# A gated message-passing kernel on one core: edge chunks of growing size, three packed lists, and six quads fetched from x

## The chip, the core and the metric

The kernel runs on one core of one Trainium2 chip. The metric is device time in microseconds, as a median of runs. Lower is better.

## The reference

There are 12,500 nodes with 128 features and 400,000 edges. The edges are sorted by destination, and the destinations are denser at small numbers. Each edge has a length. An edge counts only if its length is at most 10; the lengths are drawn up to 56, so most edges drop out.

```python
rbf = exp(-(d[:, None] - centers)**2 / (2 * width**2))           # 50 centers, width 0.1
cut = 0.5 * (cos(pi * d / 10) + 1) * (d <= 10)
W   = (silu(rbf @ fw1 + fb1) @ fw2 + fb2) * cut[:, None]          # a filter for each edge
messages = (x[src] @ pw + pb) * W
agg = segment_sum(messages, dst)
h   = x + (silu(agg @ mw1 + mb1) @ mw2 + mb2)
out = layernorm(x + h)
```

Everything is float32.

## The kernel before

The engines are VectorE (DVE), ScalarE (ACT), TensorE (PE), GpSimd (POOL) and SyncE (SP, which here only issues DMAs). The order of each engine's instructions is the order in which the kernel is written down (`manual_schedule`); no scheduler moves anything. Each engine then runs its own queue in order, and waits where it needs another one's result.

**The projection.** `x @ pw + pb` is computed once for all nodes, in 25 tiles of 512 rows, and written to a table `proj` in DRAM. For each tile SP loads x (`load_x`), PE transposes it (`turn`, L469), ACT copies the transpose out of PSUM (L471), PE multiplies it (`project`, L239 for the bias and L242), ACT copies the result (L480), and SP stores it. The bias is a sum of three bfloat16 parts, which DVE makes in `in_parts` (L229 to L233).

**Packing.** The edges that count must be brought together. The list of 400,000 edges is cut into 5 chunks. A chunk is 128 rows of 625 consecutive edges. `pack(c)` is a generator that writes down DVE instructions and yields their estimated microseconds, so that the kernel can put them between others. For one chunk DVE marks the edges that drop out (`drop`, L302), counts them along each row (`gone`, L305), and has PE add up the counts of the rows in front (`at`, L314 and L316), to know where each row's edges begin. Then it moves the edges that stay to the left, by a power of two in each of ten steps: `go` (L345) is a mask, `nodes` (L351 to L358) are node numbers and `r_d` (L360) are lengths. The front of each row becomes `line` (L365 to L380, `CAP` = 160 edges wide). POOL scatters all lines with one indirect DMA into `packed` in DRAM (L382). Neighbouring rows overlap there, so even rows go to one list and odd rows to a second; both start as zeros, and are joined by a bitwise OR. The joined list comes back as `pair` (L393). From it DVE and PE make, for each packed edge, its source (`srci`), its destination inside a window of 128 nodes (`dl`), its cutoff (`cut`) and the first node of its window (`base_i`); the lengths go to `near_d`. This is the pair stage, L401 to L456.

**The main loop.** The packed edges are worked off in 141 quads of 512. `QB` says which quads come from which chunk. For one quad:

- `fetch`: POOL issues four indirect DMAs of 128 rows from `proj` into `got` (L490). There are 8 such buffers. A fetch is written down `AHEAD` = 3 quads ahead of its use.
- `radial_of` loads the lengths (SP), `basis` makes the radial functions (ACT), `first` multiplies them by fw1 (PE, L529), `tanh` (ACT) and `silu` (DVE, L542) follow, for two quads at a time; `second` multiplies by fw2 (PE, L554).
- `message`: DVE multiplies the filter by the fetched rows (L560).
- `place`: DVE builds a one-hot matrix weighted with the cutoff (four `hot`, L568).
- `sum_up`: PE multiplies messages by it (L577), and `add` adds two windows to `aggT` (DVE, L595). `aggT` holds the whole sum in SBUF and is cleared by POOL in 25 memsets (L153).

Between these steps the loop writes down packing of later chunks, by a budget of 1.3 estimated microseconds after an even quad and 2.5 after an odd one. A yield of -3 or -1 means that the chunk rests for that many quads, while a DMA is under way. From quad 70 on, tiles of nodes that are complete get the last layers (`nodes`), and `finish` does the rest after the loop.

**Before the loop.** POOL writes the zeros of `packed` (four DMAs, L146) and clears 3,500 columns of `aggT` (7 memsets). DVE makes the parts of pb and then packs chunk 0; the 18 other memsets stand on POOL behind chunk 0's scatter. PE and ACT do the projection meanwhile. The first fetch needs both the sources of chunk 0 and the whole table `proj`.

The functions that the diff touches, with the line numbers of the profile:

Of the kernel before, what the change touches and what calls it, by code (L numbers as in the profile page):

```python
# [30 lines left out]
CAP = 160  # L31


QB = (0, 26, 54, 81, 109, 141)
NC_ = len(QB) - 1
NQ = QB[-1]
AHEAD = 3
GOT = 8
# [7 lines left out]
def kernel(  # L46
# [40 lines left out]
    R = E // (NC_ * P)  # L87
# [3 lines left out]
    assert H == P and E == NC_ * P * R and E % P == 0 and W <= N <= 1 << SB  # L91
    assert CAP <= R < 1 << (32 - RB - SB) and 2 * MW % P == 0
# [32 lines left out]
    def load_rows(c):  # L125

        raw[c] = []
        for name, ap, dt in (("r_d", edge_weight, I32), ("r_dst", dst, I32), ("r_src", src, I32)):
            t = work.tile([P, R], dt, name=name, bufs=2)
            v = ap[c * P * R:(c + 1) * P * R].rearrange("(r l) -> r l", r=P)  # L130
            nc.sync.dma_start(t, v if ap is not edge_weight else v.bitcast(I32))
            raw[c].append(t)
# [9 lines left out]
    zero_i = keep.tile([P, 2 * MW // (4 * P)], I32, name="zero_i")  # L142
    nc.gpsimd.memset(zero_i, 0)
    packed = dram.tile([2, MW], I32, name="packed")
    for k in range(4):
        nc.gpsimd.dma_start(packed.rearrange("s (k w) -> (s k) w", k=P // 2)  # L146
                            .rearrange("p (q w) -> p q w", q=4)[:, k], zero_i)
    aggT = keep.tile([P, N], F32, name="aggT")

    def clear(a, b):  # L150

        for n0 in range(a, b, 500):
            nc.gpsimd.memset(aggT[:, n0:min(n0 + 500, b)], 0.0)  # L153

    clear(0, 3500)
# [50 lines left out]
    side_i = keep.tile([P, 1], I32, name="side_i")  # L206
    nc.vector.tensor_scalar(side_i, part_i, 1, None, op0=OP.bitwise_and)
    side = keep.tile([P, 1], F32, name="side")
    nc.vector.tensor_scalar(side, side_i, float(MW), None, op0=OP.mult)
# [77 lines left out]
    bits = (R - 1).bit_length()  # L287
    LB = RB + SB

    def rowed(dt, name, n=R, bufs=1):  # L290
        return work.tile([P, n], dt, name=name, bufs=bufs)

    def pack(c):

        if c + 1 < NC_:
            load_rows(c + 1)
        r_d, r_dst, r_src = raw[c]
# [5 lines left out]
        yield 0.6  # L303
        gone = rowed(F32, "gone")
        nc.vector.tensor_tensor_scan(gone, drop, drop, 0.0, op0=OP.add, op1=OP.max)  # L305
        yield 1.4
# [4 lines left out]
        yield 0.9  # L311
# [10 lines left out]
        yield 0.6  # L322
        relc = rowed(F32, "drop")
        nc.vector.tensor_scalar(relc, rel, -127.5, None, op0=OP.add)
        yield 0.4
        nc.vector.tensor_reduce(span[:, c:c + 1], relc, AX.X, OP.max, apply_absolute_value=True)
        yield 0.7
# [4 lines left out]
        yield 0.3  # L332
# [3 lines left out]
        yield 0.7  # L336
        nc.vector.scalar_tensor_tensor(nodes, step, LB, nodes, op0=OP.logical_shift_left,
                                       op1=OP.bitwise_or)
        yield 0.7
        for b in range(bits):  # L340
            k = 1 << b

            n = min(R - k, CAP + sum(1 << j for j in range(b + 1, bits)))
            go = rowed(I32, "go")
            nc.vector.tensor_scalar(go[:, :n + k], nodes[:, :n + k], 31 - LB - b, 31,  # L345
                                    op0=OP.logical_shift_left, op1=OP.arith_shift_right)
            yield 0.4
            m = go[:, k:n + k]
            if b < bits - 1:
                after = rowed(I32, "nodes", bufs=2)  # L350
                nc.vector.scalar_tensor_tensor(after[:, :n + k], go[:, :n + k], -1,  # L351
                                               nodes[:, :n + k], op0=OP.bitwise_xor,
                                               op1=OP.bitwise_and)
                yield 0.7
                nc.vector.copy_predicated(after[:, :n], m, nodes[:, k:n + k])  # L355
                nodes = after
            else:
                nc.vector.copy_predicated(nodes[:, :n], m, nodes[:, k:n + k])  # L358
            yield 0.7
            nc.vector.copy_predicated(r_d[:, :n], m, r_d[:, k:n + k])  # L360
            yield 0.7
# [15 lines left out]
        line = work.tile([P, CAP, 2], I32, name="line", bufs=2)  # L377
# [8 lines left out]
        if c == 0:  # L386
            clear(3500, N)
        yield -3
# [3 lines left out]
        pair = work.tile([64, 2, 512], I32, name="pair", bufs=1)  # L392
# [4 lines left out]
        def paired(dt, name):  # L397
            return work.tile([64, 256], dt, name=name, bufs=1)[:np_]

        length = paired(I32, "length")  # L400
        nc.vector.tensor_tensor(length, pair[:np_, 0, 1::2], pair[:np_, 1, 1::2], OP.bitwise_or)  # L401
# [3 lines left out]
        nc.vector.tensor_tensor(two, pair[:np_, 0, ::2], pair[:np_, 1, ::2], OP.bitwise_or)  # L405
# [17 lines left out]
        def to_places(k, f, to):  # L423
            for j in range(2):
                nc.tensor.transpose(tp[:, k, j, :np_], f[:, j * P:(j + 1) * P], ident[:np_, :np_])
            nc.vector.tensor_copy(to[:, p0:p0 + np_, :].rearrange("p r j -> p j r"),
                                  tp[:, k, :, :np_])

        to_places(0, f_src, srci)
        part = paired(I32, "part")  # L430
# [32 lines left out]
    def turn(t0):  # L463
        r = rows(t0)
        n = sum(r)
        xp = bank("pu")
        x4 = x_sb.pop(t0)
        for k, m in enumerate(r):
            nc.tensor.transpose(xp[:, k * P:k * P + m], x4[:m, k, :], ident[:m, :m])  # L469
        xT = work.tile([P, 4 * P], F32, name="xT", bufs=3)  # L470
        nc.scalar.copy(xT[:, :n], xp[:, :n])  # L471
        xT_of[t0] = xT
# [9 lines left out]


    d_of, rbf_of, ph_of, t_of, s_of, pu_of, got_of, pa_of, hot_of = ({} for _ in range(9))

    def fetch(q, idx=None):
        got = work.tile([P, QT, H], F32, name="got", bufs=GOT)
        for j in range(QT):
            i = srci[:, 2 * q + j // 2, j % 2:j % 2 + 1] if idx is None else idx[:, j:j + 1]
            nc.gpsimd.indirect_dma_start(  # L490
                out=got[:, j, :], out_offset=None, in_=proj,
                in_offset=bass.IndirectOffsetOnAxis(ap=i, axis=0))
        got_of[q] = got
# [12 lines left out]
    def radial_of(o, eng=None):  # L506
        if 2 * o < NQ:
            assert all(chunk_of(q) in stored for q in quads(o))
            radial(o, [near_d[2 * q:2 * q + 2].rearrange("(o p) e -> o (p e)", o=1)
                       for q in quads(o)], eng)  # L510

    def chunk_of(q):
        return max(c for c in range(NC_) if QB[c] <= q)
# [269 lines left out]

    in_parts("pb", pb_f)
    tiles = list(range(0, NT, 4))
    turn(tiles[0])
    turn(tiles[1])
    at_t = 0.0
    weights = None
    for k, t0 in enumerate(tiles):  # L790
        if k + 6 < len(tiles):
            load_x(tiles[k + 6])
        if k == 4:
            weights = load_weights()
        project(t0)
        if k + 2 < len(tiles):
            turn(tiles[k + 2])
        t = 1.9 * (k + 1)
        while at_t < t:
            c = 0 if not rest[0] else 1  # L800
            v = next(chunks[c])
            if v < 0:
                rest[c] = -v
            else:
                at_t += 1.15 * v
    fb2_f, mb1_f, mb2_f, fw2_sb, mw1_sb, mw2_sb = weights
    rest[0] = 0
    assert not rest[1]
    advance(0, 0.1)
    fw2_h = keep.tile([H, H], F32, name="fw2_h")  # L810
    nc.vector.tensor_scalar(fw2_h, fw2_sb, 0.5, None, op0=OP.mult)
    advance(0, 1.15)
    for o in range(2):
        radial_of(o, nc.gpsimd)
    for q in range(AHEAD):
        fetch(q)
    for o in range(2, 4):
        radial_of(o)
    while 0 in todo:
        advance(0, 1.0)  # L820
    basis(0)
    first(0)
    in_parts("fb2", fb2_f)
# [10 lines left out]
    for q in range(NQ):  # L834
        nodes(q)
        if q + AHEAD < NQ:
            assert min(todo, default=NC_) > chunk_of(q + AHEAD)
            fetch(q + AHEAD)
        if q % 2 == 0:
            radial_of(q // 2 + 4)  # L840
            if 2 * (q // 2 + 1) < NQ:
                tanh(q // 2 + 1)
        else:
            if q + 3 < NQ:
                first((q + 3) // 2)
            if q + 5 < NQ:
                basis((q + 5) // 2)
        if q + 1 < NQ:
            second(q + 1)
        msg = message(q)  # L850
        sum_up(q, msg)
        if q:
            base_of(q - 1, (0,))
        if q + 1 < NQ:
            place(q + 1)
        if q:
            base_of(q - 1, (1,))
            add(q - 1)
        if q % 2 == 0 and 2 * (q // 2 + 1) < NQ:
            silu(q // 2 + 1)  # L860
        left = 1.3 if q % 2 == 0 else 2.5
        for c in list(todo[:2]):
            if rest[c]:
                rest[c] -= 1
            elif left > 0:
                left = advance(c, left)
        if not todo and "mw2" not in late:
            late["mw2"] = mw2_h = keep.tile([H, H], F32, name="mw2_h")
            nc.vector.tensor_scalar(mw2_h, mw2_sb, 0.5, None, op0=OP.mult)
            in_parts("mb1", mb1_f)  # L870
            in_parts("mb2", mb2_f)
            count()
        elif not todo and total is None:
            total = nc.values_load(bad_i[0:1, 0:1], min_val=0, max_val=2 * E)
# [86 lines left out]
```

## Time and profile before

| | us |
|---|---|
| median of 3 runs (lowest, highest) | 834.27 (833.3, 835.0) |
| the profiled execution, its own time | 830.76 |
| its span, first to last instruction | 829.0 |
| DVE busy | 679.6 (82%) |
| PE busy | 588.0 (71%) |
| POOL busy | 578.6 (70%) |
| ACT busy | 257.6 (31%) |

The span is what the profile divides up; 1.8 us of the execution lie around it. Busy time leaves out the issue of DMAs by SP and the pause that POOL makes between two gathers, so a POOL that is never free shows some 75% in the loop.

### The profile page before, as it was taken

What the parts mean: (1) busy time and instruction counts of PE and PEld (TensorE: products, weight loads), DVE (VectorE), ACT (ScalarE), POOL (GpSimd) and SP (SyncE); (2) the same over time, 40 slices, a digit from 0 to 9 for tenths busy, and PEclk for the clock granted to TensorE, in tenths of its full rate; (3) what the DMA queues carried; (4) which work ended last, traced back from release to release, by engine and by line L of the source; (5) the groups of instructions that cost most, each with busy time, mean ns of one, the idle gap of its engine ahead of it and who ended that gap; (6) DMA issues with size and microseconds to landing.
All of it is one profiled execution on the core that took longest, in us unless ns stands there. A gap on an engine that the chain in (4) does not pass through costs nothing.

```text
span 829.0 us, 11346 instructions
## 1 busy us (share of the span) xinstructions
PE 588.0 (71%) x3356; PEld 449.8 (54%) x3356; DVE 679.6 (82%) x1822; ACT 257.6 (31%) x397; POOL 578.6 (70%) x613
## 2 busy tenths in 40 slices
PE   4792766666667766776767687787877876867862
PEld 4680545455555555555555465555655664646651
DVE  7967899989999998999968888777867667667774
ACT  2454322132222322232222233523434424521521
POOL 3045777777777777777777777777777777777750
PEclk9995788878887788768896799998999988999887
DMA  8994324232153323233333442722623623632421
GB/s 245 265 309 122 96 64 128 72 103 76 49 151 77 90 73 80 58 97 88 88 83 92 102 118 77 195 66 78 181 77 89 169 80 87 171 99 52 122 61 41
DMA packets 85700, 90.62 MB, mean 109 GB/s; under 512 B 13623, under 2 KB 64851, under 8 KB 85632
## 3 DMA queue, kind: packets, MB, share of 16 engines
q1 hardware_dynamic: 66464, 49.95, 21.1%
q0 software_dynamic: 18912, 39.77, 19.4%
q8 instruction: 28, 0.46, 0.2%
q14 instruction: 40, 0.33, 0.1%
q10 hardware_dynamic: 256, 0.11, 0.1%
HBM read 74.71 MB, written 15.07 MB: 108 GB/s over the span
## 4 chain that ended last, share of the span: by engine, by line
DVE 33%; POOL 17%; PE 16%; DMA 15%; issue 14%; DVEq 3%; ACT 1%; SPq 1%; POOLq 0%; ACTq 0%
POOL got L490 16%; DMA got<-proj,srci 11%; DVE hot L568 8%; DVE s L542 4%; PE pa L577 4%; DVE msg L560 3%; DVE aggT L595 3%; PE ph L529 3%; PE pu L554 3%; DMA x<-in_x_dram 3%; DVEq L585 2%; DVE r_d L360 2%; PE pa L242 1%; PE ms L242 1%; DVE st L629 1%
## 5 line engine op out<-in xcount | busy, mean ns | idle before, releaser
L490 POOL DMA_INDIRECT got<-proj,srci x564 | 553.8, 982 | 171.9 <-issue 146.6
L577 PE MATMUL pa<-hot,msg 128*128 128x128 f32 x1128 | 184.6, 315 | 107.1 <-DVE msg L560 106.8
L577 PEld LDWEIGHTS pa<-hot,msg 128*128 128x128 f32 x1128 | 164.3, 224 | 121.4 <-DVE msg L560 121.3
L554 PEld LDWEIGHTS pu<-fw_h,s 128*128 128x128 f32 x1128 | 176.2, 223 | 12.0 <-issue 5.1
L554 PE MATMUL pu<-fw_h,s 128*128 128x128 f32 x1128 | 174.8, 306 | 0.0
L568 DVE TENSOR_SCALAR hot<-iota_n,dl,cut 128x128 f32<-128x128 f32 x564 | 158.0, 356 | 0.8 <-PE pa L577 0.6
L535 ACT ACTIVATE t<-ph 128x1024 f32<-128x1024 f32 (+1 forms) x71 | 71.8, 1012 | 268.5 <-PE ph L529 255.0
L529 PE MATMUL ph<-rbf,w_sb 51*128 51x512 f32 x282 | 101.3, 791 | 63.9 <-DVE s L542 53.3
L560 DVE TENSOR_TENSOR msg<-pu,got 128x512 f32<-128x512 f32 x141 | 96.3, 683 | 60.4 <-DMA got<-proj,srci 49.1
L542 DVE SCALAR_TENSOR_TENSOR s<-t,ph 128x1024 f32<-128x1024 f32 (+1 forms) x71 | 85.7, 1207 | 6.8 <-ACT t L535 6.7
L595 DVE TENSOR_TENSOR aggT<-aggT,pa 128x128 f32 x282 | 79.9, 283 | 7.5 <-PE ms L607 2.3
L529 PEld LDWEIGHTS ph<-rbf,w_sb 51*128 51x128 f32 x282 | 27.8, 224 | 85.3 <-issue 52.6
L551 PE MATMUL pu<-fb_b,ones_b 96*128 96x512 bf16 x141 | 61.7, 438 | 0.0
L609 ACT ACTIVATE zt<-ms 128x512 f32<-128x512 f32 (+1 forms) x25 | 14.6, 587 | 150.3 <-PE ms L607 150.3
L519 ACT ACTIVATE rbf<-d,rbf_bias,rbf_scale 128x512 f32<-128x512 f32 (+1 forms) x71 | 57.1, 804 | 0.2
L668 ACT ACTIVATE x<-x,by,rs 128x128 f32<-128x128 f32 x91 | 37.3, 482 | 59.4 <-DVE by L638 59.4
L551 PEld LDWEIGHTS <-ones_b 96*128 96x128 bf16 x141 | 14.9, 105 | 73.7 <-issue 73.2
L520 ACT ACTIVATE rbf<-rbf 128x512 f32<-128x512 f32 (+1 forms) x71 | 44.7, 630 | 2.2
L351 DVE SCALAR_TENSOR_TENSOR nodes<-go,nodes 128x625 int32<-128x625 int32 x45 | 36.5, 810 | 1.3
L360 DVE COPY_PREDICATED r_d<-go,r_d 128x624 int32<-128x624 int32 (+9 forms) x50 | 36.9, 739 | 0.0
L355 DVE COPY_PREDICATED nodes<-go,nodes 128x624 int32<-128x624 int32 (+8 forms) x45 | 35.9, 798 | 1.2
L626 DVE SCALAR_TENSOR_TENSOR x<-x,ms 128x512 f32<-128x512 f32 x23 | 15.8, 686 | 24.9 <-PE ms L242 24.9
(159 smaller groups left out, 501.1 us busy)
## 6 DMA issues: line engine op xcount, KB each, us to landing
d<-near_d SPq DMA_DIRECT2D x137, 128.0 KB
x<-in_x_dram SPq DMA_DIRECT2D x48, 256.0 KB
got<-proj,srci POOLq DMA_INDIRECT x564
proj<-hp SPq DMA_DIRECT2D x24, 256.0 KB
out_dram<-x SPq DMA_DIRECT2D x24, 256.0 KB
r_d<-in_edge_weight_dram SPq DMA_DIRECT2D x5, 312.5 KB
r_dst<-in_dst_dram SPq DMA_DIRECT2D x5, 312.5 KB
r_src<-in_src_dram SPq DMA_DIRECT2D x5, 312.5 KB
```

Source lines behind the costliest of these rows:

```text
L360: nc.vector.copy_predicated(r_d[:, :n], m, r_d[:, k:n + k])
L490: nc.gpsimd.indirect_dma_start(out=got[:, j, :], out_offset=None, in_=proj, in_offset=bass.IndirectOffsetOnAxis(ap=i, axis=0))
L519: nc.scalar.activation(rbf[:u], d[:u], AF.Square, bias=rbf_bias[:u], scale=rbf_scale[:u])
L529: nc.tensor.matmul(ph[:, h, :], w1_sb[p0:p0 + KR], rbf[p0:p0 + KR], start=True, stop=True)
L535: nc.scalar.activation(t[:, :n], ph[:, :n], AF.Tanh, scale=0.5)
L542: nc.vector.scalar_tensor_tensor(s[:, :n], t_of.pop(o)[:, :n], 1.0, ph[:, :n], op0=OP.add, op1=OP.mult)
L551: nc.tensor.matmul(pu, ones_b[:, :P], bias_b["fb2"].rearrange("k j f -> k (j f)"), start=True, stop=False)
L554: nc.tensor.matmul(pu[:, j * H:(j + 1) * H], s[:, j * P:(j + 1) * P], fw2_h, start=False, stop=(j == QT - 1))
L560: nc.vector.tensor_mul(msg, pu_of.pop(q).rearrange("p (j f) -> p j f", j=QT), got_of.pop(q))
L568: nc.vector.tensor_scalar(hot[:, j, :], iota_n[:, :W], dl[:, at[0], at[1]], cut[:, at[0], at[1]], op0=OP.is_equal, op1=OP.mult)
L577: nc.tensor.matmul(pa[:, k * W:(k + 1) * W], msg[:, j, :], hot[:, j, :], start=(j % 2 == 0), stop=(j % 2 == 1))
L595: nc.vector.tensor_add(to, to, pa[:, k * W:(k + 1) * W])
```

## The change

- The 5 equal chunks become 6, of 250, 450, 550, 625, 625 and 625 edges a row (`ROWS`), with lines of 80, 128 and then 160 edges (`CAPS`). `QB` gives them 10, 20, 24, 27, 28 and 32 quads. Smaller chunks need 8 or 9 shifting steps instead of 10.
- `packed` has three lists instead of two: row p goes to list p mod 3. The pair stage has one OR more.
- All of `aggT` is cleared by POOL at the start (25 memsets), ahead of the first scatter. The zeros of `packed` are written in three parts: a first one by POOL at the start, a second and a third by SP, late in the projection and in the loop.
- Chunk 0 is begun ahead of pb's parts. The first `FROM_X` = 6 quads are fetched from x instead of `proj`, as soon as chunk 0's sources are there. `multiply(q)` then turns the fetched rows, multiplies them by pw and adds pb, in place: for quads 0 to 3 between the projection's tiles, for quads 4 and 5 in the loop's first iterations. Quads 6 and 7 are fetched from `proj` ahead of the loop; from quad 8 on a fetch is written down 3 quads ahead, as before.
- Packing during the projection follows a written clock (2.0 us a tile on PE), and takes in chunk 0, chunk 1 up to its scatter, and the beginning of chunk 2. In the loop the budget is 4.0 while chunk 1 is unfinished, and then 1.5 and 2.9. The estimates of each operation are now worked out from its width.
- Lengths are loaded by SP whenever their chunk is stored (`radials`).

The core of the diff:

```diff
-CAP = 160
-QB = (0, 26, 54, 81, 109, 141)
+ROWS = (250, 450, 550, 625, 625, 625)
+CAPS = (80, 128, 160, 160, 160, 160)
+QB = (0, 10, 30, 54, 81, 109, 141)
+FROM_X = 6
...
-    zero_i = keep.tile([P, 2 * MW // (4 * P)], I32, name="zero_i")
+    zero_i = keep.tile([P, 376], I32, name="zero_i")
...
-    packed = dram.tile([2, MW], I32, name="packed")
-    for k in range(4):
-        nc.gpsimd.dma_start(packed.rearrange("s (k w) -> (s k) w", k=P // 2)
-                            .rearrange("p (q w) -> p q w", q=4)[:, k], zero_i)
+    packed = dram.tile([3, MW], I32, name="packed")
+    def clear_packed(k, eng):
+        a, b = CLEAR[k:k + 2]
+        for i in range(3):
+            v = packed[i, a:b].rearrange("(p w) -> p w", p=P)
+            for w0 in range(0, (b - a) // P, 376):
+                n = min(376, (b - a) // P - w0)
+                eng.dma_start(v[:, w0:w0 + n], zero_i[:, :n])
+    clear_packed(0, nc.gpsimd)
...
-    clear(0, 3500)
+    clear(0, N)
...
     def pack(c):
-        if c + 1 < NC_:
+        if 0 < c < NC_ - 1:
             load_rows(c + 1)
...
-        if c == 0:
-            clear(3500, N)
-        yield -3
+        if c:
+            yield -3
...
-        nc.vector.tensor_tensor(length, pair[:np_, 0, 1::2], pair[:np_, 1, 1::2], OP.bitwise_or)
+        nc.vector.tensor_tensor(pair[:np_, 0], pair[:np_, 0], pair[:np_, 1], OP.bitwise_or)
+        yield 0.6
+        nc.vector.tensor_tensor(length, pair[:np_, 0, 1::2], pair[:np_, 2, 1::2], OP.bitwise_or)
...
         to_places(0, f_src, srci)
+        if c == 0:
+            for q in range(FROM_X):
+                fetch(q, table=x)
...
+    def multiply(q):
+        turn("got", got_of[q])
+        h = bank("pa").rearrange("p (k f) -> p k f", k=4)
+        rows_times(h, xT_of.pop("got"), pw_sb, bias_b["pb"], [P] * 4)
+        nc.scalar.copy(got_of[q], h)
...
+    clock = 5.5
+    awake = [0.0] * NC_
+    while clock < 7.5:
+        clock += next(chunks[0])
     in_parts("pb", pb_f)
-    tiles = list(range(0, NT, 4))
+    clock += 3.5
     turn(tiles[0])
     turn(tiles[1])
...
+        if k == 3:
+            load_rows(1)
+        if k == 14:
+            radials(3)
+            in_parts("fb2", fb2_f)
...
+        if k == 20:
+            clear_packed(1, nc.sync)
         project(t0)
         if k + 2 < len(tiles):
             turn(tiles[k + 2])
-        t = 1.9 * (k + 1)
...
+        if k in (16, 18, 21, 23):
+            multiply((16, 18, 21, 23).index(k))
+        pe = 14.0 + 2.0 * k
+        while clock < pe:
...
-    for q in range(AHEAD):
+    for q in range(FROM_X, GOT):
         fetch(q)
...
         nodes(q)
-        if q + AHEAD < NQ:
+        if 4 <= q + 3 < FROM_X:
+            multiply(q + 3)
+        if GOT <= q + AHEAD < NQ:
             assert min(todo, default=NC_) > chunk_of(q + AHEAD)
             fetch(q + AHEAD)
...
-        left = 1.3 if q % 2 == 0 else 2.5
+        if q == 4:
+            clear_packed(2, nc.sync)
+        left = 4.0 if 1 in todo else 1.5 if q % 2 == 0 else 2.9
```

## The prediction

> **What bounds the kernel now.** I read the page's costliest groups first, then the timelines of POOL and DVE from the start to the loop and around the last scatter, then the busy table by stage. All times are microseconds from the span's start. The groups give POOL's gathers:
>
> ```profile
> L490 POOL DMA_INDIRECT got<-proj,srci x564 | 553.8, 982 | 171.9 <-issue 146.6
> L560 DVE TENSOR_TENSOR msg<-pu,got 128x512 f32<-128x512 f32 x141 | 96.3, 683 | 60.4 <-DMA got<-proj,srci 49.1
> ```
>
> A gather takes 0.94 to 0.98, and 0.30 of issue lies between two: 1.25 each, 5.0 a quad. POOL's timeline (start, duration, instruction):
>
> ```profile
> 5.09 3.27 POOL L153 MEMSET aggT<- 128x500 f32 x7
> 48.95 1.06 POOL L382 DMA_INDIRECT packed<-line,at_i  x1 [40.59 <-DVE first L300]
> 50.01 8.29 POOL L153 MEMSET aggT<- 128x500 f32 x18
> ...
> 71.60 1.18 POOL L490 DMA_INDIRECT got<-proj,srci  x1 [0.30 <-DVE part L277]
> ...
> 420.20 0.98 POOL L382 DMA_INDIRECT packed<-line,at_i  x1 [0.30 <-DVE aggT L595]
> 421.49 0.96 POOL L490 DMA_INDIRECT got<-proj,srci  x1 [0.30 <-issue]
> ...
> 801.92 0.94 POOL L490 DMA_INDIRECT got<-proj,srci  x1 [0.30 <-issue]
> ```
>
> From 71.6 to 802.9 POOL never pauses: 564 gathers in 731.3. The last scatter (420.2) has 304 gathers, 76 quads, behind it: 381.4, or 5.018 a quad. After the last gather come 26.1 of tail. The end is thus read off POOL, but DVE runs beside it with little to spare:
>
> ```profile
> core 0: us, PE busy (x) PEld busy (x) DVE busy (x) ACT busy (x) POOL busy (x), PEclk, DMA share, GB/s
> 90.00:150.00 60.00, 39.92 (x228) 30.84 (x226) 56.94 (x136) 14.12 (x18) 46.28 (x46) 0.83 0.35 94
> 150.00:250.00 100.00, 68.95 (x359) 52.14 (x358) 94.97 (x228) 24.14 (x30) 77.15 (x76) 0.80 0.33 87
> 250.00:350.00 100.00, 71.69 (x366) 55.35 (x365) 93.50 (x229) 26.15 (x32) 76.90 (x76) 0.77 0.29 75
> 650.00:750.00 100.00, 76.00 (x451) 57.99 (x449) 69.39 (x201) 33.52 (x54) 75.64 (x80) 0.90 0.43 111
> ```
>
> While chunks are packed DVE is 94% to 95% busy; afterwards 69%. POOL's queue is in order, and each scatter in it waits for a line that DVE packs. So far this wait costs nothing, by a small margin: DVE has the last line ready at 412.0 (row below) and POOL comes to it at 420.2.
>
> ```profile
> 6.07 2.38 DVE L229 CAST pb_p<-pb_f 96x128 bf16<-96x128 f32 x1 [1.13 <-DMA pb_f<-in_L_gnn_pb_dram]
> 8.99 0.22 DVE L229 CAST pb_p<-pb_f 96x128 bf16<-96x128 f32 x1
> ...
> 85.73 0.69 DVE L560 TENSOR_TENSOR msg<-pu,got 128x512 f32<-128x512 f32 x1 [3.50 <-PE pu L554]
> ...
> 411.68 0.32 DVE L380 TENSOR_TENSOR line<-r_d,there 128x160 int32<-128x160 int32 x1
> ```
>
> **The change, part by part.** The first gather comes earlier, but it is not what sets the end. POOL's new queue is: scatter 0, 24 gathers from x, scatter 1, 7 quads, scatter 2, 16 quads, scatter 3, 16, scatter 4, 16, scatter 5, 80 quads. In DVE's new queue 58 messages stand before the last line. So the end is the time of that line, plus 1.4 (scatter), plus 80 x 5.018 = 401.4, plus 26.1. I need the time of the line: the first message, plus DVE's work from there.
>
> *DVE's work from first message to last line.* A quad costs DVE 2.80 by its starts in the timeline: message 0.60, four hots 1.09, two adds 0.53, half a silu 0.58. A chunk of 625 costs 6.8 ahead of its bits, 26.3 for ten bits (3.0 each at full width: 0.52 + 0.84 + 0.75 + 0.87), 1.9 for the line, 7.2 for the pair stage; the third list adds an OR of 512 elements, 0.7 (the 625-wide shift-and-OR at 0.84, scaled). Scaled by width, 550 columns need 23.6 for ten bits. Behind the first message stand: pair stage of chunk 1, 7.9; chunk 2 from its nodes on, 1.5 + 23.6 + 1.9 + 7.9 = 34.9; chunks 3 and 4, 42.9 each; chunk 5 to its line, 34.9 (rounded). Together 163.4, and 57.2 quads of 2.80 are 160.1: 323.5. The same sum for before gives 319.4 against 326.2 in the trace (85.73 to 411.9): the rest is waits for PE's counts and transposes. With one more pair stage I add 8.0: 331.5. So packing that is left for the loop did not shrink: the columns done ahead of it are made up for by a sixth chunk's fixed cost and by chunk 1's pair stage. But 4 more quads now lie behind the last scatter.
>
> *The first message.* Before it stand the projection, then one chain of basis, first, tanh, silu, second: 73.97 to 85.73, 11.8, which is kept. So the question is when ACT has done its last copy of the projection.
>
> All 25 memsets of aggT now stand in front of the first scatter instead of 7. At 0.467 each (3.27/7) they run from 4.4 to 16.1 (the smaller zero writes save 0.7). The 2.38 row above is a cast that takes 0.22 elsewhere: it began under the 7 memsets and ended at 8.45, as they ended at 8.36. The Trainium skill (SBUF — State Buffer, "Who interferes with whom") says that GpSimd and a VectorE tensor_scalar, copy or cast in a two-port mode lock each other out, and that the lock is held for one instruction. By that rule DVE should get in after at most one memset, 0.53; by the row it waits for the whole run of them. I take the row. DVE's first wide tensor_scalar (drop, 250 wide), due at about 5.6, then runs at 16.1. Behind it on DVE: chunk 0's count, pb's three parts, all of chunk 0. Who waits: PE, whose very first instruction is now chunk 0's count product, and whose first projection needs pb: 16.1 + 2.3 (chunk 0's first eight operations) + 2.4 (pb) = 20.9, against 13.4 now. By the rule it would stay at about 13.4.
>
> Chunk 0 costs DVE 18.4 from drop to line (eight bits of 1.57, 0.3 + 0.4 + 0.4 + 0.5, the last ones narrow): line at 34.5. From scatter to the pair's load took 5.2 for chunk 1 (139.75 to 144.91); with the load some 9.5, so pair at 44, sources at 47 instead of 68.3: first gather at 47, 24.6 earlier. PE takes 1.55 a tile where nothing stalls (40 to 50 us). Twelve tiles from 20.9 are done at 40; PE's in-order queue then holds chunk 0's transposes, which wait for DVE: 46.2, two more to 48.4. Thirteen tiles (the last short) at 1.55 and four multiplications of gathered rows, 1.55 each, give 74.3; last copy at 75.0. (Data to move in that stretch, some 16 MB, is 52 at 310 GB/s: beside it, not more.) First message 75.0 + 11.8 = 86.8, against 85.7.
>
> *Sum.* Last line 86.8 + 331.5 = 418.3, against 412.0 now. Span 418.3 + 1.4 + 401.4 + 26.1 = 847.2. With 1.8 around the span: 849.0, against the profiled execution's 830.8: +18.2. The median shown (834.3) is 3.5 above that execution, so I say 852.
>
> *Costed at nothing.* The sixth scatter on POOL (1.3): POOL is waiting for lines anyway, reaching each with 16 quads of 5.3 plus 1.4 = 86, where DVE needs about 90; without this cover +1.3. Multiplications 4 and 5 in the loop (PE 1.55, two ACT copies 0.59 each): early iterations last 6 to 8 on DVE; without cover +4. SP: loading chunk 3 waits for chunk 1's line (about 74) with the last projection stores queued behind it, so quad 6 is fetched at about 80; its message comes after 125. The zero writes on SP (six in iteration 4) stand in front of distance loads five quads ahead. DMA load of 52 GB/s by gathers under the projection is bounded by 0 and by the whole 1.6 MB at 270 GB/s, 6; I take 0, as PE waits for DVE there, and keep 6 for the range.
>
> **Rivals.** *The lock lasts one memset* (the skill's rule). Sources at 40, projection at PE's pace with today's DMA stalls plus four multiplications, last copy 69; first message 80.8, span 841.2, so 846. For it: the wording of the skill; against it: the 2.38 row. *Faster: POOL's earlier start carries through.* If no scatter waits, 731.3 from 40 is 771, span 797, so 802. It decides at the last line: before 400.1 (829.0 - 26.1 - 401.4 - 1.4) the change gains microsecond for microsecond, so the first message would have to come at 68.6. PE's work alone (13.4 + 25 x 1.55 + 6.2) ends at 58.4 without one stall, and 1.1 + 11.8 on top is 71.3; only an overestimate of DVE's work could do it, and the margin of 8.2 at 412.0 speaks for some slack. *The projection becomes bound by DMA*: at the 270 GB/s of the first 66 us, 16 MB from 20.9 ends at 80 to 83, first message 94, span 855, so 860. *The change doesn't do what it says*: gathers from x start no earlier than 71.6. The sum would hardly change, since POOL waits for DVE's lines afterwards; it is contained in the cases above.
>
> **How the numbers follow.** Forecast 0.61, one-memset lock 0.19, DMA-bound projection 0.10, POOL carries through 0.07, all errors cancelling 0.03. The range 839 to 861 takes in the rule's case with 7 to spare, and the DMA case; the faster case is left out. About 0.2% (1.7) is what a measurement of this kernel tells from no change: faster 0.07, same 0.03, slower 0.90.
>
> **What would show it.** Right: drop's first instance ends near 16 and PE's first projection is near 21; the first gather is at 40 to 50; the first message at 84 to 90; POOL waits for DVE several microseconds at scatters 2 to 5; the last scatter is near 418 with 320 gathers after it. Wrong: POOL without pauses at its scatters, a last line before 400, or a first message before 70.

## The result, and the profile after

The changed kernel takes 854.49 us (median of 4 runs, 853.47 to 859.66); the kernel before takes 834.63 beside it (4 runs, 833.30 to 836.26). The ratio is 1.0249, with a 95% interval of 1.0204 to 1.0295 (ratios are taken over all the runs, here and below, so they are not quite the quotients of the medians). The profiled execution took 853.47, its span 851.7; the span before was 829.0. The prediction said 852 for the time and 847.2 for the span. In the experiments e1 to e4 and e6 to e10 every kernel, the one before included, took a median of 1,105 to 1,176 us, because of stalls from some 55 to 90 us on whose cause the profile does not name; of those runs I use only what lies ahead of the stalls and, with reserve, the ratio to the kernel before on the same chip.

The start, from the timelines of POOL, DVE, PE and ACT of the changed kernel (start, duration, engine, instruction, count, and in brackets the idle time before it and what ended it):

```profile
4.40 11.50 POOL L166 MEMSET aggT<- 128x500 f32 x25
5.53 10.52 DVE L328 TENSOR_SCALAR drop<-r_d 128x250 f32<-128x250 f32 x1
20.52 0.58 PE L255 MATMUL pa<-pb_b,ones_b 96*128 96x512 bf16 x1 [1.12 <-DVE pb_b L246]
34.45 0.23 DVE L406 TENSOR_TENSOR line<-r_d,there 128x80 int32<-128x80 int32 x1
...
51.64 0.20 DVE L453 CAST srci<-ms 128x40 int32<-128x40 f32 x1 [5.33 <-PE ms L452]
...
84.51 0.43 ACT L511 COPY hp<-pa 128x128 f32<-128x128 f32 x2
96.56 0.69 DVE L604 TENSOR_TENSOR msg<-pu,got 128x512 f32<-128x512 f32 x1 [3.50 <-PE pu L598]
```

An instruction that takes some 0.28 where nothing holds it (e1 and e2 below) lasts 10.52: it ends at 16.05, just after POOL's 25 memsets (15.9). PE's first projection comes at 20.5, against 13.4 before:

```profile
13.44 0.63 PE L239 MATMUL pa<-pb_b,ones_b 96*128 96x512 bf16 x1
```

And the first message comes at 96.6, against 85.7, although the first gather has been issued at 52.1 instead of 71.6.

POOL's timeline, reduced to its first gather, every pause of more than 0.4 after it, and its last gather:

```profile
52.12 1.03 POOL L528 DMA_INDIRECT got<-in_x_dram,srci  x1 [5.91 <-DVE part L461]
...
90.18 0.96 POOL L528 DMA_INDIRECT got<-proj,srci  x1 [4.36 <-DMA d<-near_d]
...
123.88 0.94 POOL L528 DMA_INDIRECT got<-proj,srci  x1 [12.77 <-issue]
...
158.50 0.99 POOL L408 DMA_INDIRECT packed<-line,at_i  x1 [19.29 <-DVE line L406]
...
248.09 1.03 POOL L408 DMA_INDIRECT packed<-line,at_i  x1 [3.80 <-DVE first L326]
...
335.31 1.03 POOL L408 DMA_INDIRECT packed<-line,at_i  x1 [1.18 <-DVE first L326]
...
422.77 0.98 POOL L408 DMA_INDIRECT packed<-line,at_i  x1 [1.18 <-DVE line L406]
...
824.99 0.94 POOL L528 DMA_INDIRECT got<-proj,srci  x1 [0.30 <-issue]
```

These numbers add up to the whole loss. Before, POOL needs 731.3 from first to last gather and never pauses; one more scatter makes that 732.6. Now it needs 773.8 (52.12 to 825.93). The six pauses between the first and the last row, each less the usual 0.30, are 40.8 of the 41.2 between the two. POOL starts 19.5 earlier, loses 41.2 in pauses and 1.3 by the scatter: +23.0, and the span has grown by 22.7. The four scatters wait for lines that DVE packs. The 12.77 is a wait for DVE too, though the profile names nothing for it: chunk 0 now holds only quads 0 to 9, so quad 10 needs chunk 1's sources. DVE makes these at 122.9, behind the messages of four quads:

```profile
118.12 0.69 DVE L604 TENSOR_TENSOR msg<-pu,got 128x512 f32<-128x512 f32 x1
118.72 1.11 DVE L612 TENSOR_SCALAR hot<-iota_n,dl,cut 128x128 f32<-128x128 f32 x4
119.75 0.61 DVE L639 TENSOR_TENSOR aggT<-aggT,pa 128x128 f32 x2
120.28 0.68 DVE L426 TENSOR_TENSOR pair<-pair 40x512 int32<-40x512 int32 x1
...
122.90 0.24 DVE L453 CAST srci<-ms 128x80 int32<-128x80 f32 x1 [0.52 <-PE ms L452]
```

The 4.36 is no wait for DVE. Quad 6 is the first that is fetched from `proj`, and ACT has copied that table's last tile only at 84.9; the DMA that the profile names loads something else. In e12 below the last copy ends at 78.9, and this gather follows its scatter with the usual 0.30.

The table by stage shows how busy DVE is while POOL waits for it (busy time of PE, PE's loads, DVE, ACT, POOL, then PE's clock, DMA share, GB/s):

```profile
core 0: us, PE busy (x) PEld busy (x) DVE busy (x) ACT busy (x) POOL busy (x), PEclk, DMA share, GB/s
40.00:50.00 10.00, 6.18 (x29) 4.32 (x28) 6.00 (x13) 3.22 (x6) 0.57 (x1) 0.73 1.01 302
...
150.00:250.00 100.00, 71.03 (x370) 54.83 (x369) 96.01 (x237) 24.15 (x30) 67.88 (x67) 0.79 0.31 81
250.00:350.00 100.00, 69.55 (x364) 53.19 (x365) 96.08 (x233) 24.15 (x30) 76.44 (x75) 0.80 0.36 95
```

DVE is 96% busy from 150 to 350, where it was 94% to 95% before; POOL's 67.88 in the first of these rows was 77.15.

### The profile page after: what moved, and what is told of

It is laid out like the page before. It is cut to its first block, busy times and chain, and to the rows that moved or that the text cites. A ratio compares the mean times of both kernels' runs of the same rounds, so it can differ in the third digit from the quotient of the medians.

```text
span 851.7 us, 11651 instructions
## 1 busy us (share of the span) xinstructions
PE 599.0 (70%) x3446; PEld 455.9 (54%) x3446; DVE 701.3 (82%) x1901; ACT 267.0 (31%) x412; POOL 577.1 (68%) x609
## 3 DMA queue, kind: packets, MB, share of 16 engines
q0 software_dynamic: 18528, 38.21, 18.2%
## 4 chain that ended last, share of the span: by engine, by line
DVE 33%; POOL 21%; issue 18%; PE 11%; DMA 10%; DVEq 3%; ACT 2%; SPq 0%; POOLq 0%
POOL got L528 21%; DMA got<-proj,srci 9%; DVE hot L612 6%; DVE s L586 4%; DVE msg L604 3%; PE pa L621 3%; DVE aggT L639 2%; DVEq L629 2%; PE ph L573 2%; DVE nodes L377 2%; DVE r_d L386 2%; DVE go L371 1%; PE pu L598 1%; DVE drop L328 1%; PE ms L258 1%
## 5 line engine op out<-in xcount | busy, mean ns | idle before, releaser
L528 POOL DMA_INDIRECT got<-proj,srci x540 | 529.5, 981 | 181.1 <-issue 154.5
L621 PE MATMUL pa<-hot,msg 128*128 128x128 f32 x1128 | 178.8, 309 | 113.9 <-DVE msg L604 113.9
L621 PEld LDWEIGHTS pa<-hot,msg 128*128 128x128 f32 x1128 | 158.8, 217 | 127.6 <-DVE msg L604 123.7
L598 PE MATMUL pu<-fw_h,s 128*128 128x128 f32 x1128 | 172.8, 304 | 0.0
L258 PEld LDWEIGHTS pa<-pw_sb,xT 128*128 128x128 f32 x244 | 33.6, 204 | 14.3 <-ACT xT L502 13.5
L258 PE MATMUL pa<-pw_sb,xT 128*128 128x128 f32 x244 | 35.7, 292 | 4.0 <-ACT xT L502 3.6
L377 DVE SCALAR_TENSOR_TENSOR nodes<-go,nodes 128x625 int32<-128x625 int32 (+3 forms) x51 | 36.5, 715 | 1.8
L381 DVE COPY_PREDICATED nodes<-go,nodes 128x624 int32<-128x624 int32 (+32 forms) x51 | 36.1, 708 | 1.4
```

The source lines that it names most:

```text
L258: nc.tensor.matmul(to[:m, k, :], lT[:, k * P:k * P + m], w, start=False, stop=(k == a + c - 1))
L528: nc.gpsimd.indirect_dma_start(out=got[:, j, :], out_offset=None, in_=proj if table is None else table, in_offset=bass.IndirectOffsetOnAxi ...
L598: nc.tensor.matmul(pu[:, j * H:(j + 1) * H], s[:, j * P:(j + 1) * P], fw2_h, start=False, stop=(j == QT - 1))
L621: nc.tensor.matmul(pa[:, k * W:(k + 1) * W], msg[:, j, :], hot[:, j, :], start=(j % 2 == 0), stop=(j % 2 == 1))
```

## Experiments

Two questions: does the held instruction at the start come from the unbroken run of memsets, and what is it worth? And is the rest POOL waiting for DVE's lists, with too few quads fetched ahead of each scatter?

**e1_gaps: a one-column memset behind each memset.** It writes zeros again and waits for the memset before it, so that POOL's queue pauses.

```diff
             nc.gpsimd.memset(aggT[:, n0:n1], 0.0)
+            nc.gpsimd.memset(aggT[:, n1 - 1:n1], 0.0)
```

> Behind each of the 25 memsets of aggT stands a memset of one of its columns, which waits for it, so POOL pauses between memsets. Theory (a memset holds VectorE's two-port instructions out, and back-to-back memsets leave no gap for them): drop takes under 1.2 us instead of 10.5, chunk 0's line is ready at 24 to 28 instead of 34.7, the first message comes at 86 to 92 instead of 96.6, the span falls to 842 to 848. Rival 1 (VectorE stays out until the whole series is done, gaps or not): drop still ends with the last memset, now at 18 to 24, and the span grows by 2 to 8. Rival 2 (drop waits for its data, not for POOL): drop still ends at 16, the span stays at 851.

Timelines of POOL and DVE in e1_gaps:

```profile
4.40 0.54 POOL L167 MEMSET aggT<- 128x500 f32 x1
5.00 0.10 POOL L168 MEMSET aggT<- 128x1 f32 x1
5.03 0.51 POOL L167 MEMSET aggT<- 128x500 f32 x1
5.60 0.23 POOL L168 MEMSET aggT<- 128x1 f32 x1
...
5.52 0.27 DVE L330 TENSOR_SCALAR drop<-r_d 128x250 f32<-128x250 f32 x1
...
7.00 0.61 DVE L349 TENSOR_SCALAR rel<-r_dst,first 128x250 int32<-128x250 int32 x1
```

POOL is busy with memsets until 19.7, and yet the instruction takes 0.27 instead of 10.52: it gets in at the pause at 5.54, and the small memset that is due there lasts 0.23 instead of 0.10. A later one (`rel`, 0.34 after the change) takes 0.61, about half a memset more. So it is not memsets beside it that hold it for 10 us, but a run of them without a pause. Chunk 0's line is ready at 27.0, as expected. (Its single run took 1146.3, against 1138.93 before; the first message, at 112 instead of 86 to 92, already lies behind stalls.)

**e2_spread, e6_spread, e10_spread: one memset at the start, the other 24 behind the 24 gathers from x.**

```diff
-    clear(0, N)
+    clear(0, 500)
+    uncleared = list(range(500, N, 500))
...
+            if uncleared:
+                n0 = uncleared.pop(0)
+                clear(n0, min(n0 + 500, N))
```

> One memset of aggT at the start, the other 24 one behind each of the 24 gathers from x. Theory: drop takes 0.3 us, chunk 0's line is ready at 24 to 26, the whole start moves up by 7 to 10, the first message comes at 86 to 90, the last line at 412 to 416, the span is 841 to 845, the time 843 to 847 (ratio to before 1.011 to 1.016). Rival (the projection is bound by its DMA traffic, and sets the first message): chunk 0 is earlier, but the first message stays at 94 to 97 and the time at 852 to 855 (1.022 to 1.026).

> One memset of aggT at the start, the other 24 one behind each of the 24 gathers from x. Theory: drop takes 0.3 us instead of 10.5, chunk 0's line is ready at 24 to 26 instead of 34.7, the first message comes at 86 to 90 instead of 96.6, the last line at 412 to 416 instead of 422.5, the span is 841 to 845, the time 843 to 847 (ratio to before 1.011 to 1.016). Rival (the projection is bound by its DMA traffic, and sets the first message): chunk 0 is earlier, but the first message stays at 94 to 97 and the time at 852 to 855 (1.022 to 1.026).

> One memset of aggT at the start, the other 24 one behind each of the 24 gathers from x. Theory: drop takes 0.3 us instead of 10.5, chunk 0's line is ready at 24 to 26 instead of 34.7, the first message comes at 86 to 90 instead of 96.6, the last line at 412 to 416 instead of 422.5, POOL waits for VectorE at the later scatters as before, 80 quads stand behind the last, the span is 841 to 845. Rival (the scatters' waits take up what the start gains): the first message is earlier, but the last line stays at 420 to 423 and the span at 849 to 852.

In all three chunk 0's line is ready at 24.4 instead of 34.7. The first gather comes at 43.4, 43.0 and 43.5 (after the change 52.1), the first message at 87.0, 88.7 and 87.0 (96.6). Ratios to before: 0.9894 (0.9831 to 0.9958) and 0.9891 (0.9839 to 0.9944); e10 was one run, 1130.46 against 1142.92. What the edit is worth where nothing stalls is left to e12.

**e5_before_clear: the kernel before, with all 25 memsets at the start and nothing else changed.**

```diff
-    clear(0, 3500)
+    clear(0, N)
...
-        if c == 0:
-            clear(3500, N)
```

> The kernel before with one part of the change alone: all 25 memsets of aggT at the start, none behind chunk 0's scatter. Theory (an unbroken run of memsets holds VectorE's two-port instructions out until it ends): pb's first cast ends at 16 to 17 instead of 8.5, chunk 0's line is ready at 56 to 57 instead of 48.7, PE's first projection starts near 21 instead of 13.4; the pair's load no longer stands behind 18 memsets, which gives back 4; the first gather comes at 75 to 78 instead of 71.6, and since POOL never waits afterwards the span grows by 3 to 7, to 832 to 836. Rival (the lock costs at most one memset): the cast ends at 6.8, the first gather comes at 66 to 68, the span falls by 3 to 5, to 824 to 826.

Timelines of DVE, PE and POOL in e5_before_clear:

```profile
6.19 10.47 DVE L229 CAST pb_p<-pb_f 96x128 bf16<-96x128 f32 x1 [1.25 <-DMA pb_f<-in_L_gnn_pb_dram]
...
18.68 0.58 PE L239 MATMUL pa<-pb_b,ones_b 96*128 96x512 bf16 x1 [5.08 <-DVE pb_b L230]
...
75.52 1.17 POOL L488 DMA_INDIRECT got<-proj,srci  x1 [0.30 <-DVE part L277]
```

The cast takes 10.47 instead of 2.38, and PE's first projection moves from 13.4 to 18.7. The first gather comes at 75.5 (71.6) and the first message at 89.5 (85.7). Two details came earlier than expected: PE's projection (near 21) and chunk 0's line (54.4, not 56 to 57). The run took 837.93 against 833.70 beside it, span 836.2. The span is just above the 832 to 836 expected, and far from the rival's 824 to 826. It is one run each, so the 4.2 of time is rough; it agrees with the 3.9 by which POOL starts later, as POOL waits at no scatter here.

**e3_ahead5 and e7_ahead5; e4_budget and e8_budget; e9_all.** Fetch 5 quads ahead; give list work less time behind each pair of quads; both together with e2's edit. The budget edit also pins two later preparations to quad 64.

```diff
-AHEAD = 3
+AHEAD = 5
...
-        left = 4.0 if 1 in todo else 1.5 if q % 2 == 0 else 2.9
+        left = 4.0 if 1 in todo else 1.0 if q % 2 == 0 else 1.9
```

> AHEAD is 5 instead of 3: in POOL's queue two more quads of gathers stand in front of each scatter from the second on; VectorE's order is the same. Theory (the end is the last line, plus the gathers queued behind the last scatter): POOL waits 9 to 11 instead of 19.3 at scatter 2, the last line stays at 422 to 423, 78 quads instead of 80 stand behind it, the span falls by 10 to 841 to 843, the time is 843 to 846 (1.010 to 1.015). Rival (POOL paces the loop by itself, its waits at the scatters are made up for later, or the 8 buffers hold it back instead): no change beyond 2 us, 852 to 856.

> AHEAD is 5 instead of 3: in POOL's queue two more quads of gathers stand in front of each scatter from the second on; VectorE's order is the same. Theory (the end is the last line, plus the gathers queued behind the last scatter): POOL waits 9 to 11 instead of 19.3 at scatter 2, the last line stays at 422 to 423, 78 quads instead of 80 stand behind it, the span falls by 10 to 841 to 843, the time is 843 to 846 (1.010 to 1.015). Rival (POOL paces the loop by itself, its waits at the scatters are made up for later, or the 8 buffers hold it back instead): no change beyond 2 us, 852 to 856.

> The loop's packing budget is 1.0 and 1.9 instead of 1.5 and 2.9 once chunk 1 is done (the node layers' constants are made in iteration 64 instead of behind the last chunk). Theory: packing reaches further into the loop, the last line comes at about 506 instead of 422.5, but only 60 quads instead of 80 stand behind it; VectorE then needs 4.6 a quad, less than POOL, so POOL waits at scatter 2 alone (16 us) and the span falls by 8 to 842 to 846, the time to 844 to 848 (1.011 to 1.017). Rival 1 (what counts is when the last line is ready): the span grows by over 20. Rival 2 (VectorE's total work bounds the kernel): no change, since the work is the same, 852 to 856.

> The loop's packing budget is 1.0 and 1.9 instead of 1.5 and 2.9 once chunk 1 is done (the node layers' constants are made in iteration 64 instead of behind the last chunk). Theory: packing reaches further into the loop, the last line comes at about 506 instead of 422.5, but only 60 quads instead of 80 stand behind it; VectorE then needs 4.6 a quad, less than POOL, so POOL waits at scatter 2 alone (16 us) and the span falls by 8 to 842 to 846, the time to 844 to 848 (1.011 to 1.017). Rival 1 (what counts is when the last line is ready): the span grows by over 20. Rival 2 (VectorE's total work bounds the kernel): no change, since the work is the same, 852 to 856.

> The three edits together: memsets spread behind the gathers from x, AHEAD 5, and the loop's budget at 1.0 and 1.9. Theory: first message at 86 to 90, POOL waits 4 to 8 at scatter 2 and nowhere else, the last line comes at 480 to 495 with 58 to 60 quads behind it, and POOL then paces to the end: last gather at 798 to 803, span 823 to 829, time 825 to 831, ratio to before 0.988 to 0.996. Rival (the three act on the same wait, so that their gains don't add): span 834 to 842, no faster than before.

Ratios to before: AHEAD alone 0.9865 (0.9837 to 0.9894) and 0.9924 (0.9897 to 0.9951); budget alone 1.0092 (1.0053 to 1.0131) and 1.0290 (1.0240 to 1.0341); all three 0.9646 (0.9577 to 0.9715). All of these runs stalled, and the expectations in microseconds don't apply; nor was the kernel after the change run beside them. They are inconclusive on what AHEAD and the budget do by themselves; they only gave the reason to repeat the last one.

**e11_all: the three edits together, without the stalls.**

> All three edits together: one memset of the accumulator at the start and 24 behind the gathers from x, AHEAD 5 instead of 3, and smaller left-over budgets per pair of quads (1.0/1.9 instead of 4.0/1.5/2.9). Theory (POOL is late by the held drop and by the four scatters that wait on VectorE's lists, and by too few quads fetched ahead of them): first gather near 43.5, first message 87 to 89, scatters 2 to 5 wait some 10 us or more but with some 83 quads already fetched before the last one instead of 61, so fewer than 60 gathers' worth of quads after it; span 823 to 829, time 825 to 831. Rival (VectorE bounds: its sum from first message to the last line is what decides and it is only moved): span 834 to 842, time 836 to 844.

It takes 826.64 (10 runs) against 835.02 (13 runs): 0.9914, with 0.9885 to 0.9942. Span 823.5. POOL's timeline in e11_all, first gather, pauses over 0.4, the last three scatters and the last gather, and DVE's last line:

```profile
42.25 1.03 POOL L529 DMA_INDIRECT got<-in_x_dram,srci  x1 [6.25 <-DVE part L462]
...
114.33 0.94 POOL L529 DMA_INDIRECT got<-proj,srci  x1 [8.33 <-issue]
...
154.26 0.99 POOL L409 DMA_INDIRECT packed<-line,at_i  x1 [4.03 <-DVE line L407]
...
272.10 0.99 POOL L409 DMA_INDIRECT packed<-line,at_i  x1 [0.30 <-issue]
...
390.00 1.36 POOL L409 DMA_INDIRECT packed<-line,at_i  x1 [0.30 <-DVE nodes L378]
...
489.64 0.31 DVE L407 TENSOR_TENSOR line<-r_d,there 128x160 int32<-128x160 int32 x1
...
505.61 0.99 POOL L409 DMA_INDIRECT packed<-line,at_i  x1 [0.30 <-DVE g_i L696]
...
796.72 0.94 POOL L529 DMA_INDIRECT got<-proj,srci  x1 [0.30 <-DMA got<-proj,srci]
```

After 154.3 POOL never waits. The last line is ready at 489.9, 67 later than after the change, and POOL comes to it only at 505.6, having fetched 83 quads instead of 61. So 58 quads are behind the last scatter instead of 80, and 28 us of span are gone. The rival (DVE's sum decides, and is only moved) expected 834 to 842 and is refuted: DVE's busy time is the same but for the hold (690.1 against 701.3), and yet the span falls. How much of the 28 is due to AHEAD and how much to the budget is not shown. Of my own expectation the waits of "some 10 us or more" at the scatters did not come: scatter 2 waited 4.0, the others not at all.

**e12_spread: the memsets alone, without the stalls.**

> The memsets alone: one at the start, 24 behind the gathers from x; AHEAD and budgets as after the change. Theory (the path is first message, then VectorE's list work of 326, then 1.4 + 80 x 5.018 + 26): first gather near 43.5, first message 87 to 88 instead of 96.6, last line 411 to 416, scatters 2 to 5 wait together 50 to 90 on VectorE's lines since POOL starts 9 earlier, span 840 to 846, time 842 to 849, so still slower than before by 1.0 to 1.8%. Rival (POOL's start decides, a microsecond of start is a microsecond of end, and the held drop is the whole loss): span 825 to 832, time as before or better.

It takes 847.46 (4 runs, 844.06 to 849.08) against 836.15: 1.0128, with 1.0088 to 1.0168. The profiled span is 847.2. DVE, PE, POOL and ACT in e12_spread:

```profile
5.53 0.27 DVE L329 TENSOR_SCALAR drop<-r_d 128x250 f32<-128x250 f32 x1
...
10.27 0.58 PE L256 MATMUL pa<-pb_b,ones_b 96*128 96x512 bf16 x1 [1.12 <-DVE pb_b L247]
...
43.48 1.04 POOL L529 DMA_INDIRECT got<-in_x_dram,srci  x1 [7.20 <-DVE part L462]
...
78.50 0.43 ACT L512 COPY hp<-pa 128x128 f32<-128x128 f32 x2
...
90.56 0.69 DVE L608 TENSOR_TENSOR msg<-pu,got 128x512 f32<-128x512 f32 x1 [3.46 <-PE pu L602]
...
152.46 0.99 POOL L409 DMA_INDIRECT packed<-line,at_i  x1 [19.28 <-DVE line L407]
...
416.56 0.32 DVE L407 TENSOR_TENSOR line<-r_d,there 128x160 int32<-128x160 int32 x1
```

Without the hold the first gather is 8.6 earlier, the first message 6.0 and the last line 5.6. The ratio goes from 2.5% above before to 1.3%, the profiled span from 22.7 above to 18.2: a half of the loss by the one and a fifth by the other, and single executions of one kernel spread over 4 to 6 us here. So the hold is a part of the loss, and not the whole of it as the rival said. POOL's start alone does not decide either: the memsets between the gathers use up its lead, so that scatter 1 is issued at 85.0, as after the change (84.8), and what is left of the gain, 4.5 of span, goes with the last line. Several numbers missed: the first message (87 to 88 expected), the last line (416.9, not 411 to 416) and the span (847.2, not 840 to 846), each by a little; and the waits at scatters 2 to 5, which were to grow to 50 to 90. They are 24.1, nearly the 25.5 of after, because POOL reaches scatter 1 no earlier.

## Why the prediction was right

**The hold at the start: right to 0.4.** The step said that drop runs at 16.1, PE's first projection at 20.9 and the line is ready at 34.5. Measured: 16.05, 20.5 and 34.7. Taking the row of 2.38 and not the rule of one instruction was right; e1 shows where the rule fits: with a pause in POOL's queue.

**The first message: 86.8 said, 96.6 measured.** This is the step that was mis-sized, and within it the last copy of the projection, said for 75.0, measured at 84.9. The chain from there (11.8) was right: 11.7. Two terms failed. "Twelve tiles from 20.9 are done at 40", transposes at 46.2: PE ends the twelfth tile at 50.9 and comes to the list's transposes at 51.3, hence the 5.33 wait of `srci` above and a first gather at 52 instead of 47. In that stretch (40 to 50, table above) DMA runs at share 1.01 and 302 GB/s while PE is busy 6.18 of 10. PE waits for ACT's copies, and these wait for stores of the table:

```profile
36.54 0.58 ACT L511 COPY hp<-pa 128x512 f32<-128x512 f32 x1 [3.75 <-DMA proj<-hp]
...
41.40 0.58 ACT L511 COPY hp<-pa 128x512 f32<-128x512 f32 x1 [3.78 <-DMA proj<-hp]
...
45.01 0.58 ACT L511 COPY hp<-pa 128x512 f32<-128x512 f32 x1 [2.54 <-DMA proj<-hp]
```

"Beside it, not more" was wrong, and the DMA-bound rival, which gave 94 for the first message, came nearer. That DMA's rate is the cause I read from these rows; no run isolates it. The hold is not the cause of this term: in e12, where PE's first projection comes 10.2 earlier, the last copy ends only 6.0 earlier, so the stretch is 68.7 there and 64.4 after the change, against the 54 forecast. "Four multiplications, 1.55 each": PE goes from the rows' transpose to the copy by ACT and on to the product without other work between, and waits for the first copy in each; the first of them:

```profile
63.00 0.60 PE L500 MATMUL pu<-ident,got 128*128 128x128 f32 x4
63.43 0.38 PE L255 MATMUL pa<-pb_b,ones_b 96*128 96x512 bf16 x1
64.42 1.16 PE L258 MATMUL pa<-pw_sb,xT 128*128 128x128 f32 x8 [0.60 <-ACT xT L502]
65.42 0.38 PE L255 MATMUL pa<-pb_b,ones_b 96*128 96x512 bf16 x1
```

63.00 to 65.42 is 2.4; the four take 2.4, 3.4, 2.4 and 2.3, together 4.3 more than said. The two terms, 5.1 and 4.3, make 9.4 of the 9.9 by which the last copy is late.

**From first message to last line: 331.5 said, 325.9 measured.** The line is DVE's:

```profile
422.17 0.32 DVE L406 TENSOR_TENSOR line<-r_d,there 128x160 int32<-128x160 int32 x1
```

The 323.5 of work is right within 1%; the allowance of 8.0 for waits was too large. Before it was 326.3, and 326.3 in e12: packing that is left for the loop did not shrink, as the step said. The stretch is not fixed, though: it is 402.9 in e11, where the packing is spread over more quads (first message 87.0).

**The rest.** 80 quads behind the last scatter: 401.9 (401.4 said), tail 25.8 (26.1). So the span's forecast was 4.5 low: +9.8 by the first message, -5.6 by the waits, and +0.3 by the rest. The 852 was close partly by luck: the first message's error and that of the waits cancel in part, and the 3.5 that was added to come to the median was 1.0 here (854.49 against 853.47), which took another 2.5 off.

**POOL's waits.** Waits "several us at scatters 2 to 5" came: 19.3, 3.8, 1.2 and 1.2; only the first two are of that size. The 12.8 for chunk 1's sources is not in the prediction. Neither is the 4.4 for the table: quad 6 was said to be fetched at about 80, and was at 90.2. They did no harm to its sum, which runs over DVE, but whoever reads off POOL needs them.

**The rivals.** "POOL carries through" failed, as said, because the first message (96.6) was far behind 68.6. Its condition, a last line before 400.1, holds only for 61 quads ahead of the last scatter. In e11 the last line comes at 489.9 and POOL does not wait for it, since 83 quads stand ahead of that scatter.

## What to carry to other kernels

Starting an in-order queue earlier is worth nothing while a later entry in it waits for another engine: find that entry, count what is queued behind it, and either make its input earlier or let more independent work go ahead of it. Work of one engine that another engine can be shut out by belongs in the pauses of its queue, not in one run at the start.

## What was not expected of the hardware

The run of memsets held VectorE only because POOL's queue did not pause. Twenty-five memsets in 11.50 (0.46 each, where one by itself takes 0.54, so they overlap) kept a VectorE tensor_scalar out for 10.52 and a cast for 10.47; with a pause of some 0.06 behind each 0.5 the same instruction took 0.27, and later ones of its kind up to 0.6 instead of 0.3. Not everything is held: a cast of 128x1 took 0.14 at 5.46, while the memsets ran without a pause, and in e1, between the memsets, the scan of 128x250 (L333) took the 0.68 that it takes after the change without any beside it.
